# Pairwise bilinear products on one core: scaling whole pairs in one ScalarE instruction, third products four halves behind, tiles kept for the run

## The chip, the cores and the metric

The kernel runs on one core of a Trainium2 chip. The measure is the device time in microseconds (us) of one execution. The profile gives the same execution instruction by instruction; its names for the engines are PE (TensorE's matmuls), PEld (TensorE's weight loads), DVE (VectorE), ACT (ScalarE), POOL (GpSimd) and SP (SyncE, which here only issues transfers).

## The reference

There are 32 fields of 128 values for each of 1024 batch rows, and a 128x128 matrix for each of the 496 pairs of fields. For each pair (i, j) with i < j, field i is multiplied by the pair's matrix, and the result element by element by field j, all in fp32.

```python
v_i = inputs[:, I_IDX, :]
v_j = inputs[:, J_IDX, :]
transformed = jnp.einsum('bpd,ped->bpe', v_i, W)
return transformed * v_j
```

The inputs are 1024x32x128 and 496x128x128 values, the output 1024x496x128 values (260 MB).

## The kernel before, in words

**Layout.** The host transposes, so that a field `xt[f]` is a tile of 128 partitions (the 128 values) by 1024 columns (the batch), and a pair's output is a 128x1024 tile too. Pairs are taken in the order of `_pairs()`: i falls from 30 to 0, and j runs from i+1 to 31. So field i is first needed as the left factor when its group of 31 - i pairs begins.

**Number formats.** The first 15 pairs (`nq0`, i from 30 to 26) are plain fp32 matmuls (L231), 512 columns each. The other 481 are made of three products in the float32r format, from operands that are split in two parts each. With `h` a slightly shrunk copy of the operand (times 1 - 2^-13), `l` the rest and `d` a combination of both, the result is (xh\*wh + xl\*wl)\*(1 + EPS) + xd\*wd. `split_x` makes `xh` (ScalarE, L159), `xl` (GpSimd, L160 and L161) and `xd` (VectorE, L298, put off through the list `later`) in halves of 512 columns. `split_w` makes `wh` (ScalarE, L141), `wl` and `wd` (GpSimd, L143 to L145) for two pairs at a time (`WC`).

**The loop.** `u` counts halves of pairs, q = u // 2 the pairs. A half's step has two parts:
- `first(u)`: the two products xh\*wh and xl\*wl (L234) into a half of the pair's PSUM tile `po`, and then ScalarE's scaling of that half in place (L236).
- `second(u - LAG)`, so for the half that is `LAG` = 3 steps back: the third product xd\*wd (L245), which adds onto the scaled values. After a pair's second half, VectorE multiplies the whole 128x1024 tile by field j into a quarter of an output tile `ot` (L255). Only the last two pairs do this by halves (L253).

A `po` tile takes up two of PSUM's banks, one for each half, and `PB` = 4 of them rotate. So a pair's first product has to wait for VectorE's product of the pair four before.

**Output.** Four pairs share an `ot` tile of 2 MB; its store is issued on ScalarE's queue (L282), two steps after the last third product (`SLAG`). Three `ot` tiles are there for the whole run. Four more (`g0` to `g3`) serve until their space is needed for fields that are loaded during the run: `XAT` names the pairs, 52, 141, 219 and 313, at which these loads begin.

**Order.** The schedule is written out by hand (`manual_schedule`): each engine takes its instructions in the order in which the loop issues them. At the end of an odd step, at most one waiting split from `todo` is issued. `apart` declares to the framework that two instructions need no wait between them. Dependencies between the accesses to a `po` tile are otherwise kept for the tile as a whole.

Of the kernel before, what the change touches and what calls it, by code (L numbers as in the profile page):

```python
# [7 lines left out]
F32 = mybir.dt.float32  # L8
F32R = mybir.dt.float32r
ALU = mybir.AluOpType  # L10

P = 128
NF = 32
NQ = NF * (NF - 1) // 2
BT = 1024
HB = 512
WC = 2
WL = 8
OG = 4
EPS = 2.0**-12  # L20
NATIVE = 5
SHARED = 26
XDLAG = 10
LAG = 3
SPREAD = 18
PB = 4
WB = 3
# [14 lines left out]
PB = 4  # L42
# [8 lines left out]
def kernel(  # L51
# [22 lines left out]
    nc = tc.nc  # L74
# [3 lines left out]
    xpool = ctx.enter_context(tc.tile_pool(name="x", bufs=1))  # L78
    spool = ctx.enter_context(tc.tile_pool(name="xs", bufs=2))
    rpool = ctx.enter_context(tc.tile_pool(name="wr", bufs=WB))  # L80
    wpool = ctx.enter_context(tc.tile_pool(name="ws", bufs=4))
    opool = ctx.enter_context(tc.tile_pool(name="o", bufs=1))
    ppool = ctx.enter_context(tc.tile_pool(name="ps", bufs=PB, space=bass.MemoryType.PSUM))

    x_sb = {}

# [15 lines left out]
    def move_on(k):  # L102

        nc.gpsimd.dma_start(out=mark[: 2 * k], in_=xt[0, : 2 * k, :16].rearrange("(b a) n -> a b n", a=k))  # L104
# [21 lines left out]

    scaled, taken, halved = {}, {}, {}

    def apart(inst, other, reason="the halves of a pair lie in two banks"):

        if other is not None:
            tc.declare_no_dep(inst.ins, other.ins, reason=reason)

    w_s, spent = {}, []

    def split_w(c, u):

        k = c * WC % WL
        raw = w_raw[c * WC // WL][:, k : k + WC, :].rearrange("p q e -> p (q e)")
        h, l, d = [wpool.tile([P, WC * P], F32R, tag=t, name=f"{t}_{c}") for t in ("wh", "wl", "wd")]  # L140
        halved[c] = nc.scalar.mul(h, raw, 1.0 - 2.0**-13)  # L141
        apart(halved[c], halved.get(c - 4), "one engine writes both, in order")
        nc.gpsimd.tensor_tensor(l, raw, h.bitcast(F32), ALU.subtract)  # L143
        nc.gpsimd.tensor_scalar(d, h.bitcast(F32), EPS, 1.0, ALU.mult, ALU.mult)  # L144
        nc.gpsimd.tensor_tensor(d, l.bitcast(F32), d.bitcast(F32), ALU.subtract)  # L145
        w_s[c] = (h, l, d)
        if (c + 1) * WC % WL == 0:
            spent.append(c * WC // WL)

    x_s = {}  # L150
    later = []

    def split_x(f, a, u):
# [10 lines left out]
        if f > NF - 2 - NATIVE - SHARED:  # L164
            later.append((min(u + XDLAG, 2 * first_q[f] + LAG - 1), d, h.bitcast(F32), l.bitcast(F32)))
        else:
# [9 lines left out]
    for c in range(c0, nchunk):  # L176
        todo.append(((c - 3) * WC + 1, max(c * WC, nq0), lambda u, c=c: split_w(c, u)))
# [35 lines left out]
    def out_tile(g):  # L213
        t = min((t for t in used if (g + 1) * OG <= until.get(t, NQ + OG)), key=used.get)
        used[t] = g
        pool = xpool if t in until else opool
        return pool.tile([P, OG, BT], F32, tag=t, name=f"ot_{g}")

    ctx.enter_context(tc.manual_schedule())
    po, ots, stores = {}, {}, []  # L220


    def first(u):
        q, h = divmod(u, 2)
        i, c = pairs[q][0], q // WC
        r = slice(q % WC * P, (q % WC + 1) * P)
        s = slice(h * HB, (h + 1) * HB)
        if h == 0:
            po[q] = ppool.tile([P, BT], F32, tag="po", name=f"po_{q}")
        if q < nq0:  # L230
            nc.tensor.matmul(po[q][:, s], w_raw[q // WL][:, q % WL, :], x_sb[i][:, s], start=True, stop=True)  # L231
        else:
            for t in (0, 1):
                m = nc.tensor.matmul(po[q][:, s], w_s[c][t][:, r], x_s[i][t][:, s], start=t == 0, stop=t == 1)  # L234
                apart(m, scaled.get(u - 1) if h else None)
            scaled[u] = nc.scalar.mul(po[q][:, s], po[q][:, s], 1.0 + EPS)  # L236
            apart(scaled[u], taken.get(q - PB), "TensorE's products, which this waits for, have waited for it")

    def second(u):
        q, h = divmod(u, 2)  # L240
        i, j = pairs[q]
        r = slice(q % WC * P, (q % WC + 1) * P)
        s = slice(h * HB, (h + 1) * HB)
        if q >= nq0:
            m = nc.tensor.matmul(  # L245
                po[q][:, s], w_s[q // WC][2][:, r], x_s[i][2][:, s], start=False, stop=True, skip_group_check=True
            )
            apart(m, scaled[u ^ 1])
        g, k = divmod(q, OG)
        if k == 0 and h == 0:  # L250
            ots[g] = out_tile(g)
        if q >= NQ - 2:
            nc.vector.tensor_tensor(ots[g][:, k, s], po[q][:, s], x_sb[j][:, s], ALU.mult)  # L253
        elif h == 1:
            taken[q] = nc.vector.tensor_tensor(ots[g][:, k, :], po.pop(q), x_sb[j], ALU.mult)  # L255
        if q >= NQ - 2:
            stores.append((u + SLAG, out[g, :, k, s], ots[g][:, k, s]))
        elif g == 0 or q >= NQ - OG:
            if h == 1:
                stores.append((u + SLAG, out[g, :, k], ots[g][:, k]))  # L260
        elif k == OG - 1 and h == 1:
            stores.append((u + SLAG, out[g], ots[g]))

    for u in range(2 * NQ + LAG + SLAG):
        q = u // 2
        if u < 2 * NQ:
            i, j = pairs[q]
            if u % 2 == 0 and j == i + 1 and XG * ngroup < i - 2 - XLEAD:
                load_x(i - 2 - XLEAD)
            first(u)  # L270
            if u == 2 * nq0:
                move_on(5)
            if u % 2 == 0 and q in group_at:
                load_group(*group_at[q])
            if u % 2 == 1 and q in w_at:
                load_w(w_at[q])
            if u % 2 == 0 and q in back:
                move_on(16 - NE if max(w_raw) < WAPART[-1] else 13)
        if LAG <= u < 2 * NQ + LAG:
            second(u - LAG)  # L280
        while stores and stores[0][0] <= u - LAG:
            nc.scalar.dma_start(*stores.pop(0)[1:])  # L282
# [5 lines left out]
        if ring[WB:] and ring[0] in spent:  # L288
            ring.pop(0)
            c = ring[WB - 1]  # L290
# [39 lines left out]
```

## Time and profile before

| | |
|---|---|
| median of 3 runs | 745.56 us (743.81, 745.56, 748.67) |
| the profiled execution's own time | 743.81 us |
| its span, first to last instruction | 742.0 us |
| busy: PE, DVE, ACT, POOL | 703.8, 636.8, 634.9, 594.8 us |
| moved | 310.04 MB, mean 418 GB/s |
| L236 scaling, 128x512 | 962 times, mean 584 ns |
| L255 product, 128x1024 | 494 times, mean 1220 to 1222 ns |
| L234 and L245 matmul, 128x512 | 2886 times, 391 to 398 ns each |
| L141 weight part, 128x256; L159 field part, 128x512 | 241 times 410 ns; 52 times 624 ns |

The profile's matmuls overlap: each is shown from its start to its modelled end, and the next one starts before that. So their pace is read from the starts, and a busy PE isn't a PE without gaps. A row of waits names the engine, tile and line that waited, what it waited for, the total in us, the number of times and the longest. In a timeline the columns are start, duration, engine, line and operation, output and inputs; a bracket gives the idle time ahead of it and what ended that.

### The profile page before, as it was taken

The numbers are of one execution on the slowest core, as the hardware profiler recorded it, in microseconds if no ns is written. First come the engines' busy times: TensorE is split into PE (matmuls) and PEld (weight loads), VectorE is DVE, ScalarE is ACT, GpSimd is POOL, SyncE is SP. The second block draws the span as 40 slices with busy tenths as digits, with TensorE's granted clock in tenths as the row PEclk, the third lists the DMA queues.
The fourth block names the chain that finished last, engine by engine and source line by source line (L and its number), as shares of the span: only waits on it lengthen the run. The fifth ranks groups of instructions, "written<-read, shape, count | busy, mean of one in ns | idle before, by whom it ended". The sixth has DMA issues, their size and how long they took to land.

```text
span 742.0 us, 10650 instructions
## 1 busy us (share of the span) xinstructions
PE 703.8 (95%) x2946; PEld 549.4 (74%) x2946; DVE 636.8 (86%) x550; ACT 634.9 (86%) x1256; POOL 594.8 (80%) x882
## 2 busy tenths in 40 slices
PE   7999999999999999999899979999999999999994
PEld 3577777777878887776687758867878778777783
DVE  4888999999999998987798868977999899888885
ACT  1298999999999999898899968988989999998893
POOL 1789999999999999887778866977797878797660
PEclk9999999999999999999999999999999999999998
DMA  9999999999999999999999998999999999999998
GB/s 347 427 424 428 427 427 425 430 423 426 427 419 426 423 424 425 425 423 422 425 428 422 428 423 334 420 423 423 423 425 422 426 423 415 430 421 422 424 408 351
DMA packets 34667, 310.04 MB, mean 418 GB/s; under 512 B 5296, under 2 KB 5424, under 8 KB 18992
## 3 DMA queue, kind: packets, MB, share of 16 engines
q10 hardware_dynamic: 19584, 261.10, 83.4%
q1 hardware_dynamic: 10592, 36.77, 12.3%
q0 software_dynamic: 4432, 11.48, 3.9%
q8 instruction: 24, 0.39, 0.2%
q14 instruction: 35, 0.29, 0.1%
HBM read 49.29 MB, written 260.05 MB: 417 GB/s over the span
## 4 chain that ended last, share of the span: by engine, by line
PE 61%; DMA 23%; DVE 8%; POOL 3%; issue 2%; ACT 1%; DVEq 0%; ACTq 0%; POOLq 0%
PE po L234 38%; DMA out_dram<-ot 23%; PE po L245 19%; DVE ot L255 6%; PE po L231 4%; DVE xd L298 2%; POOL wd L145 1%; POOL wl L143 1%; POOL xl L160 1%; ACT po L236 0%; DMA x<-in_xt_dram 0%; POOL xl L161 0%; POOL wd L144 0%; DVE ot L253 0%; ACT wh L141 0%
## 5 line engine op out<-in xcount | busy, mean ns | idle before, releaser
L236 ACT ACTIVATE po<-po 128x512 f32<-128x512 f32 x962 | 553.4, 584 | 76.3 <-PE po L234 60.3
L255 DVE TENSOR_TENSOR ot<-po,x 128x1024 f32<-128x1024 f32 x358 | 429.8, 1220 | 70.9 <-DMA out_dram<-ot 23.8
L234 PE MATMUL po<-xh,wh 128*128 128x512 f32 x962 | 382.4, 398 | 20.1 <-DVE ot L255 19.1
L245 PE MATMUL po<-xd,wd 128*128 128x512 f32 x962 | 376.3, 391 | 4.8 <-DVE ot L253 2.4
L234 PE MATMUL po<-xl,wl 128*128 128x512 f32 x962 | 377.1, 392 | 1.4 <-POOL wl L143 1.0
L234 PEld LDWEIGHTS po<-xh,wh 128*128 128x128 f32 x962 | 181.2, 188 | 78.3 <-DVE ot L255 41.7
L143 POOL TENSOR_TENSOR wl<-w,wh 128x256 fp32r<-128x256 f32 x241 | 185.2, 768 | 66.1 <-ACT wh L141 60.0
L245 PEld LDWEIGHTS po<-xd,wd 128*128 128x128 f32 x962 | 181.1, 188 | 45.2 <-DVE ot L253 3.2
L234 PEld LDWEIGHTS po<-xl,wl 128*128 128x128 f32 x962 | 181.3, 188 | 41.0 <-POOL wl L143 4.0
L145 POOL TENSOR_TENSOR wd<-wl,wd 128x256 fp32r<-128x256 f32 x241 | 181.4, 753 | 20.1
L255 DVE TENSOR_TENSOR ot<-po,x_g 128x1024 f32<-128x1024 f32 x136 | 164.0, 1222 | 25.9 <-DMA out_dram<-ot 9.7
L144 POOL TENSOR_SCALAR wd<-wh 128x256 fp32r<-128x256 f32 x241 | 101.9, 423 | 20.5
L141 ACT ACTIVATE wh<-w 128x256 fp32r<-128x256 f32 x241 | 98.7, 410 | 5.7 <-DVE ot L255 3.6
L298 DVE TENSOR_TENSOR xd<-xh,xl 128x512 fp32r<-128x512 f32 x52 | 48.5, 934 | 0.0
L160 POOL TENSOR_TENSOR xl<-x_g,xh 128x512 fp32r<-128x512 f32 x32 | 41.5, 1297 | 3.2 <-ACT xh L159 2.9
L160 POOL TENSOR_TENSOR xl<-x,xh 128x512 fp32r<-128x512 f32 x20 | 25.8, 1290 | 15.7 <-ACT xh L159 15.4
L161 POOL TENSOR_SCALAR xl<-xl 128x512 fp32r<-128x512 f32 x52 | 34.4, 662 | 4.6
L231 PE MATMUL po<-x,w 128*128 128x512 f32 x60 | 28.4, 630 | 3.9 <-DMA x<-in_xt_dram 3.9
L231 PEld LDWEIGHTS po<-x,w 128*128 128x128 f32 x60 | 11.6, 199 | 19.9 <-issue 13.7
L159 ACT ACTIVATE xh<-x 128x512 fp32r<-128x512 f32 x20 | 12.3, 624 | 11.4 <-DMA x<-in_xt_dram 11.3
L159 ACT ACTIVATE xh<-x_g 128x512 fp32r<-128x512 f32 x32 | 20.0, 624 | 0.0
L104 POOL DMA_DIRECT2D mark<-in_xt_dram x26 | 16.6, 637 | 0.0
(7 smaller groups left out, 19.9 us busy)
## 6 DMA issues: line engine op xcount, KB each, us to landing
out_dram<-ot ACTq DMA_DIRECT2D x122, 2048.0 KB, 13.2
w<-in_wt_dram SPq DMA_DIRECT2D x36, 512.0 KB, 11.1
w<-in_wt_dram POOLq DMA_DIRECT2D x25, 448.0 KB, 11.8
x_g<-in_xt_dram SPq DMA_DIRECT2D x16, 512.0 KB, 17.0
x<-in_xt_dram SPq DMA_DIRECT2D x14, 512.0 KB, 9.5
out_dram<-ot ACTq DMA_DIRECT2D x6, 512.0 KB, 8.3
w<-in_wt_dram SPq DMA_DIRECT2D x26, 64.0 KB, 6.1
x<-in_xt_dram ACTq DMA_DIRECT2D x4, 256.0 KB, 5.7
```

The costliest lines, as they stand in the source:

```text
L141: halved[c] = nc.scalar.mul(h, raw, 1.0 - 2.0**-13)
L143: nc.gpsimd.tensor_tensor(l, raw, h.bitcast(F32), ALU.subtract)
L144: nc.gpsimd.tensor_scalar(d, h.bitcast(F32), EPS, 1.0, ALU.mult, ALU.mult)
L145: nc.gpsimd.tensor_tensor(d, l.bitcast(F32), d.bitcast(F32), ALU.subtract)
L160: nc.gpsimd.tensor_tensor(l, x_sb[f][:, s], h.bitcast(F32), ALU.subtract)
L161: nc.gpsimd.tensor_scalar(l, l.bitcast(F32), 1.0 / EPS, 1.0, ALU.mult, ALU.mult)
L231: nc.tensor.matmul(po[q][:, s], w_raw[q // WL][:, q % WL, :], x_sb[i][:, s], start=True, stop=True)
L234: m = nc.tensor.matmul(po[q][:, s], w_s[c][t][:, r], x_s[i][t][:, s], start=t == 0, stop=t == 1)
L236: scaled[u] = nc.scalar.mul(po[q][:, s], po[q][:, s], 1.0 + EPS)
L245: m = nc.tensor.matmul(po[q][:, s], w_s[q // WC][2][:, r], x_s[i][2][:, s], start=False, stop=True, skip_group_check=True)
L255: taken[q] = nc.vector.tensor_tensor(ots[g][:, k, :], po.pop(q), x_sb[j], ALU.mult)
L298: nc.vector.tensor_tensor(*later.pop(0)[1:], ALU.subtract)
```

## The change

`LAG` becomes 4, and the scaling moves from each half to the pair: after the first two products of the second half, one ScalarE instruction scales the whole 128x1024 tile. The third products then come four halves behind. The four PSUM tiles and the four sets of weight parts are made once and used in turn, where before a pool handed out a new tile for each pair and each chunk. The waits between the two halves of a pair that had been declared needless are gone with the halves, and there is a new declaration: VectorE's product doesn't wait for the scaling by itself, as TensorE's third product has waited for it.

```diff
-LAG = 3
+LAG = 4
...
-    wpool = ctx.enter_context(tc.tile_pool(name="ws", bufs=4))
+    wpool = ctx.enter_context(tc.tile_pool(name="ws", bufs=1))
...
-    ppool = ctx.enter_context(tc.tile_pool(name="ps", bufs=PB, space=bass.MemoryType.PSUM))
+    ppool = ctx.enter_context(tc.tile_pool(name="ps", bufs=1, space=bass.MemoryType.PSUM))
...
+    w_t = [[wpool.tile([P, WC * P], F32R, tag=f"{t}{k}", name=f"{t}_{k}") for t in ("wh", "wl", "wd")] for k in range(4)]
...
-        h, l, d = [wpool.tile([P, WC * P], F32R, tag=t, name=f"{t}_{c}") for t in ("wh", "wl", "wd")]
+        h, l, d = w_t[c % 4]
...
+    po_t = [ppool.tile([P, BT], F32, tag=f"po{k}", name=f"po_{k}") for k in range(PB)]
...
-            po[q] = ppool.tile([P, BT], F32, tag="po", name=f"po_{q}")
+            po[q] = po_t[q % PB]
...
             for t in (0, 1):
-                m = nc.tensor.matmul(po[q][:, s], w_s[c][t][:, r], x_s[i][t][:, s], start=t == 0, stop=t == 1)
-                apart(m, scaled.get(u - 1) if h else None)
-            scaled[u] = nc.scalar.mul(po[q][:, s], po[q][:, s], 1.0 + EPS)
-            apart(scaled[u], taken.get(q - PB), "TensorE's products, which this waits for, have waited for it")
+                nc.tensor.matmul(po[q][:, s], w_s[c][t][:, r], x_s[i][t][:, s], start=t == 0, stop=t == 1)
+            if h == 1:
+                scaled[q] = nc.scalar.mul(po[q], po[q], 1.0 + EPS)
+                apart(scaled[q], taken.get(q - PB), "TensorE's products, which this waits for, have waited for it")
...
-            m = nc.tensor.matmul(
+            nc.tensor.matmul(
                 po[q][:, s], w_s[q // WC][2][:, r], x_s[i][2][:, s], start=False, stop=True, skip_group_check=True
             )
-            apart(m, scaled[u ^ 1])
...
             taken[q] = nc.vector.tensor_tensor(ots[g][:, k, :], po.pop(q), x_sb[j], ALU.mult)
+            apart(taken[q], scaled.get(q), "TensorE's product, which this waits for, has waited for it")
```

More of the change, by code (lines that the diff above doesn't have):

```diff
@@ L127, with apart @@
     scaled, taken, halved = {}, {}, {}
-    def apart(inst, other, reason="the halves of a pair lie in two banks"):
+    def apart(inst, other, reason):
         if other is not None:
```

## The prediction

> **What bounds the kernel now.** I first read the slices of the page: does one resource run flat?
>
> ```profile
> PE   7999999999999999999899979999999999999994
> ...
> ACT  1298999999999999898899968988989999998893
> ...
> DMA  9999999999999999999999998999999999999998
> GB/s 347 427 424 428 427 427 425 430 423 426 427 419 426 423 424 425 425 423 422 425 428 422 428 423 334 420 423 423 423 425 422 426 423 415 430 421 422 424 408 351
> ```
>
> The transfers do: about 425 GB/s from the second slice on. 310.04 MB at 425 GB/s are 729.5 us of the 742.0 us span. But TensorE is nearly as full, so the next view is busy time and matmul counts in stages that I chose by what changes in them (dense field splits; a waiting pipeline; the last loads; no loads).
>
> ```profile
> 50.00:290.00 240.00, 234.52 (x1007) 186.65 (x1006) 223.20 (x194) 222.51 (x445) 221.20 (x319) 1.00 1.01 425
> 290.00:500.00 210.00, 196.44 (x829) 155.10 (x828) 172.16 (x151) 181.08 (x358) 165.57 (x251) 0.98 1.00 416
> 500.00:690.00 190.00, 185.52 (x802) 148.89 (x801) 166.90 (x143) 173.50 (x344) 155.97 (x236) 1.00 1.01 423
> 690.00:731.00 41.00, 39.97 (x174) 31.96 (x172) 36.20 (x31) 36.59 (x71) 23.81 (x39) 1.00 0.98 412
> ```
>
> The columns are length, then busy us (and count) of PE, PE weight load, VectorE, ScalarE, GpSimd, then clock, DMA share, GB/s. In the timeline undisturbed matmuls start 0.2265 us apart, so a pair (six) needs 1.359 us. Counts times 0.2265 leave PE idle for 11.9, 18.8 (3.4 of its 22.2 us are a spell of about 7 us at half clock), 8.3 and 1.6 us. Compute and transfers are balanced within a few per cent. Who waits says which leads where:
>
> ```profile
> ACT po L236 <- PE po L234: 60.3, 197, 8.4
> ...
> PEld po L234 <- DVE ot L255: 41.7, 58, 5.8
> DVE ot L255 <- DMA out_dram<-ot: 33.5, 32, 6.3
> ...
> PEld po L245 <- ACT po L236: 3.2, 2, 1.6
> ...
> PE po L245 <- ACT po L236: 1.2, 1, 1.2
> ```
>
> VectorE waits for an output buffer mainly after 290 us (2.6 us in 150 to 300, 16.1, 8.2 and 6.9 later). The chain agrees: up to 292 us it is PE, VectorE and GpSimd; then stores of 12 to 21 us alternate with PE, the last landing at 690 us; from there PE and VectorE to the last products. A store issued at 293.4 lands 19.5 us later: that backlog is what compute may lose before 290 us without starving the DMA engines. Later stores land after 11 to 13 us.
>
> **What the Trainium skill says.** "ScalarE: Activation LUTs", What ACT_TABLE_LOAD costs: an ACTIVATE grows by 0.833 ns per element; here 128x256 takes 410 and 128x512 takes 624 ns, 0.836. "PSUM — Partial Sum Buffer", Specifications: eight banks of 512 fp32 values; a 1024-wide tile takes two, so four tiles are all there is, and every cycle below has four slots. "TensorE: Matmul & The Clock Gate", opening table: the queue pulls weight loads ahead of running matmuls. The trace agrees and shows the price when it can't (next fence). "DMA: Bandwidth & Descriptors", Anatomy of one DMA, fits 436 GB/s; the trace has 425.
>
> **The change, part by part.**
>
> *ScalarE.* Removed: 962 scalings of 584 ns. Added: 481 of 584 + 512 x 0.836 = 1012 ns (bounds: 584 + 512 x 0.8 and twice 584). Saved: 561.8 - 486.8 = 75 us of ScalarE. On the path this is worth little: PE's waits for ScalarE are 3.2 and 1.2 us. Can the longer scaling be late? From the second product of a pair's second half to its first third product ten matmuls pass, 2.27 us. The scaling starts 0.48 us after that product's start (705.35 to 705.84), takes 1.01, hands over in 0.05, and the weight load wants it 0.11 to 0.2 earlier: 0.5 us is left, as much as one 410 ns weight split ahead of it. So I cost it at nothing; without that cover a 624 ns field split would add 0.1 to 0.2 us, 52 times at most. The store issue, two halves behind its third product as before, now follows a whole-pair scaling: 0.4 us later, behind a backlog of over 10 us, so nothing; were there none, 0.4 us for each of the 32 waits, 13 us.
>
> *Third products four halves behind.* This is the term that counts. A PSUM tile is held from its first product, through its last third product, to the end of VectorE's product; the same slot's next first product waits for that. In PE's order, first and last were 14 matmuls apart and become 17. A slot's turn is 24 matmuls: 5.436 us. What must fit into the rest is in the timeline:
>
> ```profile
> 701.48 0.39 PE L245 MATMUL po<-xd,wd 128*128 128x512 f32 x1
> ...
> 701.64 3.52 DVE L255 TENSOR_TENSOR ot<-po,x_g 128x1024 f32<-128x1024 f32 x3 [1.23 <-PE po L234]
> ...
> 702.91 0.19 PEld L234 LDWEIGHTS po<-xh,wh 128*128 128x128 f32 x1 [0.79 <-DVE ot L255]
> 702.91 0.50 PE L234 MATMUL po<-xh,wh 128*128 128x512 f32 x1 [0.37 <-DVE ot L255]
> ...
> 703.25 0.40 PE L234 MATMUL po<-xl,wl 128*128 128x512 f32 x1
> ...
> 704.89 0.39 PE L245 MATMUL po<-xd,wd 128*128 128x512 f32 x1
> ...
> 705.32 1.23 DVE L255 TENSOR_TENSOR ot<-po,x_g 128x1024 f32<-128x1024 f32 x1 [0.17 <-PE po L245]
> ```
>
> An idle VectorE starts 0.43 us after the third product's start (704.89 to 705.32), works 1.22 and releases PE 0.05 later (702.86 to 702.91). A PE that waited loads weights only then: its next matmul comes after 0.34 instead of 0.2265, 0.113 lost. Before: 14 x 0.2265 + 1.70 + 0.113 = 4.98 us, under 5.436 with 0.45 to spare. After: 17 x 0.2265 + 1.70 + 0.113 = 5.66 us, over by 0.228. The first slot that stalls shifts the other three, which then have that slack, so one stall per four pairs: 1.416 us a pair, +0.057. Lower bound +0.029 (restart hidden: 5.55 / 4), upper +0.113 (each pair restarts).
>
> Next, what the lost slack had covered: 52 `xd` differences (L298, mean 934 ns) queue on VectorE ahead of products. At 1.416 us a pair VectorE idles 0.2, so one pushes the next product 0.73 us. If that is the stalled slot (one case in four) all reaches PE; else 0.228 twice over is absorbed and 0.27 remains. Mean 0.39, taken 0.4 (bounds 0.2, 0.73).
>
> The sum, by stage, extra against PE's idle:
> - 30 to 50 us: 14 pairs x 0.057 = +0.8.
> - 50 to 290: 168 x 0.057 + 26 x 0.4 = 20.0; PE's present 6.7 us of waits for VectorE there are the same stalls: +13.3. Backlog 19.5, so the DMA engines aren't starved.
> - 290 to 500: 138 x 0.057 + 12 x 0.4 = 12.7 in place of 18.8 idle, because a late compute no longer waits for buffers: -6.1.
> - 500 to 690: 134 x 0.057 + 10 x 0.4 = 11.6 for 8.3: +3.3.
> - 690 to the end: 29 x 0.057 = 1.7 for part of 1.6 idle, +0.8, and +0.4 for the last pair, whose third products wait for 1012 instead of 584 ns.
> Together +12.5 us. The profiled execution's own time is 743.81 (its span and 1.8 us), which gives 756.3; it was the fastest of three (median 745.56), but the slower ones may have had slower transfers, which hide the same loss, so I add nothing: 756.
>
> *The rest.* Tiles kept for the run, ScalarE's waits declared away, VectorE not waiting for ScalarE, GpSimd's `wl` not for PE: no row of the waits shows one of these ending last for more than 0.6 us. Nothing; a gain is at most that. Queue order on VectorE, GpSimd and SyncE stays, only the third products and what hangs on them move one half.
>
> **The rivals.**
> 1. Hidden. With +0.029 and 0.2 the stages give 3.4 late at 290, then 6.4 for 18.8 and 5.9 for 8.3: caught up, and only the tail's 1.2 stays: 745. For: the flat GB/s row. Against: the restart gap is plainly there.
> 2. Pile-up. At 0.73 per `xd` the stages give 0.8 + 21.9 - 2.1 + 6.6 + 1.2 = 28: 772. For: two `xd` in a row last up to 1.66 us. Against: many would fall in slack.
> 3. Not slower: ScalarE is what truly paces PE (two scalings and half a weight split are 1.37 us a pair, PE 1.359), and its store issue blocks scalings while it waits for VectorE (at 53 us PE waits 1.2 us through it). Relief brings PE's 4.4 us of waits back: 739. It decides if VectorE's turnaround with restart fits seven matmuls, 1.585 us; I read 1.81.
>
> **Numbers.** Likeliest 0.56 (750 to 765), hidden 0.24 (743 to 749), pile-up 0.14 (765 to 799), ScalarE 0.06. 744 to 770 leaves out ScalarE, a sixth of hidden and half of pile-up, 0.17. A change of 1% (7.5 us) is about what can be told from none: above 753 lie four fifths of the likeliest and the pile-up, 0.60; faster by over 1% is a third of the last, 0.02.
>
> **What would show it.** Right: PE's waits for VectorE (weight loads included) rise from some 42 us to over 70, in short ones of 0.1 to 0.8 us, also in 50 to 290 us; VectorE's waits for stores fall under 15; stores land sooner, under 9 us after 500; scalings near 1012 ns, ScalarE near 560 us busy, PE hardly waiting for it; the chain in the last 200 us is PE and VectorE without stores. Wrong: matmuls keeping 0.2265 us pace with waits for stores as now (rival 1), or third products waiting on ScalarE for tens of us, which my 0.5 us of margin would have mis-sized.

## The result, and the profile after

The changed kernel takes 772.1 us (median of 5 runs, 770.98 to 773.18) against 745.8 us (5 runs, 743.81 to 748.67): ratio 1.0348, 95% interval 1.032 to 1.0377. Slower by 3.5%, where 756 us, and 744 to 770 us as the range, had been forecast. The profiled execution took 772.05 us, its span is 770.3 us, 28.3 us more than before.

The slices of the page, again TensorE, ScalarE, transfers and GB/s:

```profile
PE   7999999999999999999999999999999999999994
...
ACT  1288878888877887878878778788878878877773
...
DMA  9999999999999999999999999999999999999988
GB/s 347 432 422 426 391 412 427 422 398 377 383 379 417 426 424 427 395 412 375 423 432 420 413 380 393 407 427 424 418 396 390 388 403 395 388 394 400 417 367 328
```

The GB/s row is no longer flat: from the second slice to the 38th it runs between 375 and 432, and the mean is 402 where it was 418. The busy row of the DMA engines still shows nines, so that row alone would have hidden that they had lost the lead. The waits (engine, what for; total us, times, longest) say who has it:

```profile
ACT po L238 <- PE po L236: 151.9, 427, 9.9
PEld po L236 <- DVE ot L256: 115.6, 356, 1.0
DVE ot L256 <- PE po L247: 102.8, 334, 2.0
```

PE's weight loads wait for VectorE 356 times instead of 58; VectorE in turn waits for PE's third products. No row is left in which VectorE waits for a store, and none in which PE waits for ScalarE. The chain that ended last, by engine, in the kernel before:

```profile
PE 61%; DMA 23%; DVE 8%; POOL 3%; issue 2%; ACT 1%; DVEq 0%; ACTq 0%; POOLq 0%
```

and in the changed kernel:

```profile
PE 75%; DVE 10%; ACT 5%; POOL 4%; DMA 2%; issue 2%; SPq 0%; ACTq 0%; POOLq 0%; DVEq 0%
```

The 23% were stores, the 2% are loads. By stages (PE's count of matmuls in its first pair of brackets):

```profile
50.00:290.00 240.00, 236.18 (x945) 167.52 (x945) 207.23 (x183) 194.77 (x260) 210.84 (x299) 1.00 1.00 407
290.00:500.00 210.00, 208.21 (x837) 148.22 (x836) 177.57 (x153) 168.17 (x222) 171.08 (x255) 1.00 1.00 407
500.00:690.00 190.00, 188.37 (x758) 133.75 (x758) 160.29 (x137) 151.86 (x200) 150.15 (x225) 1.00 1.00 402
690.00:731.00 41.00, 41.00 (x167) 28.95 (x166) 33.59 (x29) 32.04 (x43) 27.07 (x44) 1.00 1.00 410
```

PE starts 945 matmuls in the first of these stages instead of 1007; in the later ones it starts 837 instead of 829, 758 instead of 802 and 167 instead of 174. The timeline of the changed kernel shows the pattern that does it:

```profile
647.99 0.19 PEld L236 LDWEIGHTS po<-xh,wh 128*128 128x128 f32 x1 [0.36 <-DVE ot L256]
...
649.37 0.19 PEld L236 LDWEIGHTS po<-xh,wh 128*128 128x128 f32 x1 [0.16 <-DVE ot L256]
...
650.96 0.19 PEld L236 LDWEIGHTS po<-xh,wh 128*128 128x128 f32 x1 [0.38 <-DVE ot L256]
...
652.68 1.23 DVE L256 TENSOR_TENSOR ot<-po,x 128x1024 f32<-128x1024 f32 x1 [0.41 <-PE po L247]
...
653.95 0.19 PEld L236 LDWEIGHTS po<-xh,wh 128*128 128x128 f32 x1 [0.35 <-DVE ot L256]
```

The weight loads of the first products of successive pairs begin at 647.99, 649.37, 650.96 and (two pairs on) 653.95. A long wait comes in every second pair, and two pairs take 2.97 to 2.99 us. Twelve matmuls at 0.2265 us would take 2.72. The whole timeline reads the same: of all stretches from one pair's first product to that of the next pair but one, four fifths last 2.93 to 3.02 us.

### The profile page after: what moved, and what is told of

It is laid out like the page before. It is cut to its first block, busy times and chain, and to the rows that moved or that the text cites. A ratio compares the mean times of both kernels' runs of the same rounds, so it can differ in the third digit from the quotient of the medians.

```text
span 770.3 us, 8887 instructions
## 1 busy us (share of the span) xinstructions
PE 749.3 (97%) x2946; PEld 523.2 (68%) x2946; DVE 638.3 (83%) x550; ACT 587.9 (76%) x775; POOL 600.3 (78%) x882
## 4 chain that ended last, share of the span: by engine, by line
PE 75%; DVE 10%; ACT 5%; POOL 4%; DMA 2%; issue 2%; SPq 0%; ACTq 0%; POOLq 0%; DVEq 0%
PE po L236 50%; PE po L247 21%; DVE ot L256 6%; DVE xd L300 4%; ACT po L238 4%; PE po L233 4%; DMA x_g<-in_xt_dram 2%; ACT wh L142 2%; POOL xl L161 1%; POOL wd L146 1%; POOL wl L144 1%; DMA x<-in_xt_dram 1%; POOL wd L145 1%; POOL xl L162 1%; DVE ot L254 0%
## 5 line engine op out<-in xcount | busy, mean ns | idle before, releaser
L238 ACT ACTIVATE po<-po 128x1024 f32<-128x1024 f32 x481 | 485.2, 1009 | 152.3 <-PE po L236 151.9
L256 DVE TENSOR_TENSOR ot<-po,x 128x1024 f32<-128x1024 f32 x358 | 436.8, 1223 | 90.4 <-PE po L247 70.8
L236 PE MATMUL po<-xh,wh 128*128 128x512 f32 x962 | 405.5, 421 | 6.5 <-DVE ot L256 4.3
L236 PEld LDWEIGHTS po<-xh,wh 128*128 128x128 f32 x962 | 180.3, 187 | 149.5 <-DVE ot L256 115.6
L144 POOL TENSOR_TENSOR wl<-w,wh 128x256 fp32r<-128x256 f32 x241 | 193.0, 801 | 91.3 <-ACT wh L142 86.2
L256 DVE TENSOR_TENSOR ot<-po,x_g 128x1024 f32<-128x1024 f32 x136 | 166.4, 1224 | 34.3 <-PE po L247 32.1
L145 POOL TENSOR_SCALAR wd<-wh 128x256 fp32r<-128x256 f32 x241 | 100.0, 415 | 20.5
L300 DVE TENSOR_TENSOR xd<-xh,xl 128x512 fp32r<-128x512 f32 x52 | 40.6, 780 | 0.0
```

The costliest lines, as they stand in the source:

```text
L238: scaled[q] = nc.scalar.mul(po[q], po[q], 1.0 + EPS)
L300: nc.vector.tensor_tensor(*later.pop(0)[1:], ALU.subtract)
```

## What the trace says against the forecast's loop, and the theories

The forecast had the loop of the four PSUM tiles right, but let one stall in four pairs serve all four slots. That is not what this order of instructions does. In PE's order a pair n starts at position 0, the next pairs at 6, 12 and 18, its own last third product is at 17, and its tile is wanted again at 24. Stalls of the pairs n+1 and n+2 lie inside the hold and delay the tile's release just as much as they delay PE. Only a stall of the pair n+3 comes after the hold, and gives VectorE time. Call D(n) what a pair loses (the wait for its tile, and the restart after it), m the 0.2265 us of a matmul and T the turnaround (third product's start to VectorE 0.43, product 1.22, hand-over 0.05, restart 0.113: 1.81 us). Seven matmuls and D(n+3) must cover T:

D(n+4) + D(n+3) = T - 7m

So every two neighbours share the deficit; they can split it in any way, but as long as this loop sets the pace, two pairs take 12m + T - 7m = 5m + T. With 1.81 us that is 2.94 us; the trace's 2.97 makes T 1.84. Three explanations of the loss were put to the test:

- Theory A: this loop is the whole loss.
- Theory B, a rival of the forecast: the `xd` differences pile up on a VectorE without slack.
- Theory C: the loss doesn't come from the hold but from the whole-pair scaling, or from new waits that the kept tiles bring.

## The experiments

**Only the distance, in the kernel before.**

```diff
-LAG = 3
+LAG = 4
```

> The kernel before with the third products four halves behind in place of three and nothing else: scaling by halves, pools as they were. Theory A (slot loop): the loss of the whole change is the longer hold of a PSUM tile; two pairs need 5 matmuls and VectorE's turnaround T = 1.81 to 1.86 us more than the 12 matmuls allow, 1.47 to 1.50 us a pair; 766 to 774 us, with PE's weight loads waiting for VectorE over 100 us. Theory B (pile-up of the xd differences on VectorE): same time, so this run does not tell A from B. Theory C (the whole-pair scaling or the kept tiles cost it): 744 to 749 us.

Measured: 778.65 us, ratio 1.0416 (1.0376 to 1.0457). The waits of this run:

```profile
PEld po L234 <- DVE ot L255: 119.5, 344, 1.3
DVE ot L255 <- PE po L245: 103.3, 316, 2.0
```

One number alone brings the whole loss and the same waits, with scaling by halves and pools as before: theory C falls. It is even above the expected 766 to 774 us, and slower than the changed kernel: by the two ratios, whose intervals just touch, the rest of the change gives back some 0.7% once the loop binds. Two pairs again take 2.98 us in the median over the whole timeline, as in the changed kernel, so the difference lies in the fifth of the stretches that are longer than 3.02 us. What differs in the profile is the `xd` row: 950 ns in the median (46.8 us in all) where the changed kernel has 682 ns (40.6 us). Why these differences are longer, and whether they are the cause, was not settled.

**The distance undone, in the changed kernel.**

```diff
-LAG = 4
+LAG = 3
```

> The changed kernel with the third products three halves behind: whole-pair scaling and kept tiles stay. Theory A: the slot loop has its slack back, so PE's waits for VectorE fall under 50 us; but a third product now starts 7 matmuls, 1.585 us, after the product that the scaling waits for, and the scaling needs 0.48 + 1.01 + 0.05 + 0.113 = 1.65 us, so PE waits for ScalarE in nearly every pair: 1.43 to 1.46 us a pair, 747 to 760 us. Theory B: also without the loop, 745 to 750 us. Theory C: 770 us or more.

Measured: 749.72 us, ratio 1.0013 (0.9989 to 1.0036): no difference from the kernel before. The waits:

```profile
PEld po L247 <- issue: 34.8, 164, 0.3
DVE ot L256 <- DMA out_dram<-ot: 25.6, 25, 5.5
PEld po L236 <- DVE ot L256: 18.8, 29, 4.8
```

PE's weight loads wait for VectorE 18.8 us in place of 115.6, and VectorE waits for stores again. The price is that the scaling now has only 7 matmuls before the third product needs it. The timeline shows it:

```profile
708.06 1.01 ACT L238 ACTIVATE po<-po 128x1024 f32<-128x1024 f32 x1 [0.65 <-PE po L236]
...
709.18 0.19 PEld L247 LDWEIGHTS po<-xd,wd 128*128 128x128 f32 x1 [0.21 <-issue]
709.25 0.43 PE L247 MATMUL po<-xd,wd 128*128 128x512 f32 x1
```

The scaling ends at 709.07, the third product's weights load at 709.18, 0.2 us after the load unit fell idle. I read this as a wait for the scaling; the view of waits books such gaps without a releaser (34.8 us in 164 places). Over the whole timeline a pair takes 1.41 us in the median (1.36 in the kernel before), a little less than the 1.43 to 1.46 expected. This costs no time because the transfers set the pace again: stores are 17% of the chain that ended last.

**One matmul less in the hold.** The third product goes between the two first products of its step.

```diff
                 nc.tensor.matmul(po[q][:, s], w_s[c][t][:, r], x_s[i][t][:, s], start=t == 0, stop=t == 1)
+                if t == 0 and u - LAG >= 2 * nq0:
+                    second(u - LAG)
...
-        if LAG <= u < 2 * NQ + LAG:
+        if LAG <= u < 2 * NQ + LAG and not 2 * nq0 <= u - LAG < 2 * NQ - LAG:
             second(u - LAG)
```

> The changed kernel, four halves behind, with each third product put between the two first products of its step rather than behind them. A tile is held for 16 matmuls, one fewer; the scaling has 8 matmuls, 1.81 us, for its 1.65. Theory A: 8 matmuls stand against T = 1.84 us: 0.03 us lost in two pairs, so the loop no longer sets the pace; PE's weight loads wait for VectorE under 70 us, 744 to 752 us. If the loss were spread evenly over the hold (22 us for 3 matmuls), a third of it would go: 760 to 766 us. Theory B: xd differences still hit a loop without slack: 755 to 765 us.

Measured: 749.86 us, ratio 1.003 (1.0012 to 1.0048). The waits:

```profile
PEld po L236 <- DVE ot L258: 63.7, 169, 4.3
...
DVE ot L258 <- DMA out_dram<-ot: 16.2, 16, 4.3
```

The hold of 16 costs 0.3%, the hold of 17 3.5%. The loss isn't proportional to the hold; nearly all of it comes with the last matmul. Against a turnaround of 1.84 us, 8 matmuls (1.81 us) are 0.03 us short in two pairs, and 7 (1.59 us) are 0.25 us short. The timeline of this run agrees: two pairs take 2.76 us in the median, 2.72 in the kernel before. So small a deficit, an estimated 7 us in 481 pairs, can hide behind the transfers.

**Two matmuls less.** Both third products of a pair together, after the first products of an even step.

```diff
-        if LAG <= u < 2 * NQ + LAG:
+        if u % 2 == 0 and LAG <= u < 2 * NQ + LAG:
             second(u - LAG)
+            second(u - LAG + 1)
```

> The changed kernel with both third products of a pair one after the other, after the first products of the pair two later. Whole-pair scaling, kept tiles and the scaling's time of 9 matmuls (2.04 us) before the first third product stay about as they are; a tile is held 15 matmuls in place of 17. Theory A: 9 matmuls, 2.04 us, are left for a turnaround of 1.81 to 1.86 us, so the stalls go and the transfers bound it again: 741 to 748 us, PE's weight loads waiting for VectorE under 60 us. Theory B: the slack of 0.2 us is much less than an xd difference, so much of the loss stays, 755 to 765 us. Theory C: 770 us.

Measured: 749.43 us, ratio 1.0024 (1.0003 to 1.0046). The waits:

```profile
PEld po L236 <- DVE ot L256: 50.6, 68, 5.5
DVE ot L256 <- DMA out_dram<-ot: 27.9, 27, 5.7
```

PE's weight loads wait for VectorE 50.6 us (41.7 in the kernel before), and VectorE waits for stores again. The whole-pair scaling can thus be had without the loop's stall, and then it brings no gain: the transfers bound the kernel again. Slack of 0.2 us was enough, so theory B, which wanted 755 us or more, fails here.

**Without the differences.** `xd` isn't computed, and the third product reads `xl` in its place.

```diff
-            later.append((min(u + XDLAG, 2 * first_q[f] + LAG - 1), d, h.bitcast(F32), l.bitcast(F32)))
+            pass
...
-                po[q][:, s], w_s[q // WC][2][:, r], x_s[i][2][:, s], start=False, stop=True, skip_group_check=True
+                po[q][:, s], w_s[q // WC][2][:, r], x_s[i][1][:, s], start=False, stop=True, skip_group_check=True
```

> The changed kernel without the 52 xd differences on VectorE (the third product takes xl in place of xd, so this part of the computation is left out). Theory A: the loop stalls every second pair whether or not there are differences; they cost some 0.15 us each: 760 to 766 us. Theory B: back to 744 to 750 us. Theory C: 765 to 772 us.

Measured: 762.08 us, ratio 1.0194 (1.0148 to 1.0241), and

```profile
PEld po L236 <- DVE ot L256: 116.7, 420, 1.6
```

The loop's waits stay in full, and now 99% of all stretches of two pairs last 2.93 to 3.02 us. The loop alone thus leaves 18.3 us of the 28.3 (760.3 us of span against 742.0), and theory A is not quite the whole. The span falls by 10.0 us (770.3 to 760.3), 0.19 us for each of the 52 differences, so theory B holds for about a third of the loss at most. In the kernel before the same differences lie in front of VectorE too; what they cost there was not tried, so how much of the 10 us is new stays open.

**Only the kept tiles**, in the kernel before, with the new declaration for VectorE (the main lines of the edit):

```diff
-            po[q] = ppool.tile([P, BT], F32, tag="po", name=f"po_{q}")
+            po[q] = po_t[q % PB]
...
-        h, l, d = [wpool.tile([P, WC * P], F32R, tag=t, name=f"{t}_{c}") for t in ("wh", "wl", "wd")]
+        h, l, d = w_t[c % 4]
```

> The kernel before with the tiles kept for the run and VectorE's product declared free of the scaling; scaling by halves and three halves behind stay. Theory A: nothing, ratio 0.997 to 1.003 and PE's waits as before. Theory C (the kept tiles bring the waits): 755 us or more, with a new wait of PE or ScalarE.

Measured: 748.62 us, ratio 0.9998 (0.9972 to 1.0024). The kept tiles change nothing, as forecast.

**A longer hold.** `LAG = 5` in the changed kernel: 20 matmuls, 4 left.

> The changed kernel with the third products five halves behind. A tile is held for 20 matmuls of its slot's 24, so 4 matmuls, 0.906 us, are left for VectorE's turnaround of T = 1.84 us (7 matmuls and the 0.25 us that the changed kernel's trace loses in every second pair). With this hold the first products of the next three pairs all fall inside it, so no stall helps another: each pair loses T - 0.906 = 0.93 us, 2.29 us a pair, 481 pairs, with some 45 us for the start, the xd differences and the end: theory A 1130 to 1165 us. The prediction's reading (one stall in four pairs shared by all): 0.91 us in four pairs, 1.59 us a pair, about 815 us. Theory B (xd differences): 790 us or less.

Measured: 1925.09 us, far outside every expectation. The waits show a second cause:

```profile
PEld po L247 <- POOL wd L146: 611.2, 237, 3.6
PE po L247 <- POOL wd L146: 485.3, 237, 3.2
PEld po L236 <- DVE ot L256: 406.6, 477, 1.1
```

With five halves the last third product of each chunk comes in the program after the split that reuses its weight part, so it takes a later chunk's part (that much of the computation is changed) and waits for GpSimd to make it. TensorE's mean granted clock was 0.709 in this run. It therefore doesn't measure the loop alone; where only the loop held, its pairs were 2.96 us apart at a clock of 0.50 (601 to 604 us). The next run removes the second cause by issuing all splits one pair later:

```diff
-            ready = [t for t in todo if t[0] <= q]
+            ready = [t for t in todo if t[0] <= q - 1]
```

> The run at five halves behind once more, with every operand split one pair later. In the run before, the last third product of each chunk of two pairs came after the weight part that it reads had been overwritten by a later chunk's (a changed computation), and so waited for GpSimd; and TensorE ran at half clock for part of the time. Where only the loop held that run, its pairs were 2.96 us apart at half clock: 2 matmuls of 0.42 and a turnaround of 2.12 us (0.67 + 1.22 + 0.06 + 0.17). Theory A: GpSimd's waits are gone; each pair takes 2 matmuls and T, 2 x 0.2265 + 1.84 = 2.29 us at full clock and 2.96 at half; 481 pairs and 45 us: 1145 us if the clock stays full, 1470 if it is always half. The prediction's reading (one stall for four pairs) gives 815 us at full clock and some 1300 at half (6 x 0.42 + 0.1 us a pair). Theory B: under 800 us.

Measured: 1137.93 us in a single execution, clock 0.996. The timeline, first products of successive pairs:

```profile
701.39 0.50 PE L236 MATMUL po<-xh,wh 128*128 128x512 f32 x1 [0.62 <-DVE ot L256]
...
703.67 0.50 PE L236 MATMUL po<-xh,wh 128*128 128x512 f32 x1 [0.62 <-DVE ot L256]
...
705.95 0.50 PE L236 MATMUL po<-xh,wh 128*128 128x512 f32 x1 [0.63 <-DVE ot L256]
```

Every pair stalls, 2.28 us apart. With 20 matmuls the starts of all three following pairs lie in the hold, no stall helps another, and a pair takes 6m + T - 4m = 2m + T: T comes out as 1.83 us, nearly the same as at four halves behind. Theory A said 1145 us before the run; the forecast's way of reading the loop gives 815.

## Why the prediction was wrong

Right in it: that PE's wait for VectorE over the PSUM tiles takes the lead; the turnaround (1.81 us read from the kernel before, 1.83 and 1.84 in the runs); the scaling (1012 ns forecast, 1009 measured) and its harmlessness for PE; nothing from the kept tiles; waits for VectorE over 70 us (115.6) and no more waits for stores; stores landing sooner (8.9 us in the median between 500 and 700 us), and none in the chain that ended last.

The step that failed is the sentence "The first slot that stalls shifts the other three, which then have that slack, so one stall per four pairs: 1.416 us a pair, +0.057". A stall gives slack only where it falls outside the other tile's hold, and with 17 of 24 matmuls held only one of the three neighbours' does. In its place stands one deficit per two pairs: 2.97 / 2 = 1.485 us a pair, +0.126, more than double. The upper bound of +0.113 was below this as well, because it supposed a restart in each pair and no wait.

With 1.485 us a pair, a matmul started less is 0.2475 us of lateness. Stage by stage, forecast against the two traces' counts:

| stage | forecast | matmuls before, after | lateness |
|---|---|---|---|
| 30 to 50 us | +0.8 | 85, 77 | +2.0 |
| 50 to 290 | +13.3 | 1007, 945 | +15.3 |
| 290 to 500 | -6.1 | 829, 837 | -2.0 |
| 500 to 690 | +3.3 | 802, 758 | +10.9 |
| 690 to 731 | +0.8, end +0.4 | 174, 167 | +1.7 |

The right-hand column adds up to 27.9 us, the spans differ by 28.3. The miss lies where the forecast counted on the idle time that transfers had imposed: from 290 us on it left a pair 0.057 us of loss to hide, but there were 0.126. From 50 to 290 us the forecast came out closer, because two more errors went the other way. A difference on VectorE costs 0.19 us (the run without them), not 0.4, and just below the lower bound of 0.2; the differences had also become shorter, 780 ns in the mean for 934. And the forecast let the new stalls take the place of only 6.7 of the 11.9 us that PE had been idle there. The stage now has 945 matmuls, so 158 pairs, and 25 differences: 158 x 0.126 + 25 x 0.19 = 24.7 us, of the 26.0 us that PE is idle (240 less 945 x 0.2265). So nearly all of the former idle time has gone into the new stalls.

Rival 1, hidden, is refuted by the GB/s row. Rival 2 named 772 us, which is the time, but that is a coincidence: without any `xd` the kernel still takes 762 us. Rival 3 fails on its own condition: the turnaround doesn't fit seven matmuls. Its other half can be judged from the runs with a shorter hold: a relieved ScalarE brings nothing measurable there. ScalarE's busy time fell from 634.9 to 587.9 us, by 47 and not 75: the scalings fell from 561.8 to 485.2 us, but before, instructions of 693 us in sum (561.8, 241 x 0.410 and 52 x 0.624) had filled only 634.9 us of busy time, so they had overlapped.

## What to carry to other kernels

When a ring of buffers is used in turn by two in-order engines, write down the positions at which the holds begin and end in the producer's order; a stall inside a hold lengthens it, and only the starts after the hold's end share the deficit. The period follows from that (here 5m + T for two pairs), and so does where the loss begins: with one matmul less in the hold, the same turnaround cost 0.3%. Before an engine's work is made cheaper at the price of a longer hold, look at which engine reads the ring's buffers last, and at how much of the turn is left for it.

## What the runs showed of the hardware that was not expected

- A DMA busy share of 1 doesn't show that the transfers set the pace: from 50 to 290 us it reads 1.01 at 425 GB/s before, and still 1.00 at 407 GB/s after.
- Short pauses in every pair did not lower PE's clock. In the last run at five halves behind, PE paused 0.62 us in each pair of 2.28 us and kept a mean clock of 0.996 (one execution). In the run before it, PE also waited for GpSimd in 237 places, 485.3 us in all, so about 2 us each, and its mean clock was 0.709. The 3.2 us come at the start; from 60 us to 1900 us its timeline shows no pause longer than 2.3 us, yet the clock falls to 0.50 in stretches. Which length or share of pauses sets the clock down was not tried.
